# Two stages of one kernel rewritten: the order of pair attention's weights (with two memory tiles for them), and the Fourier stage's last part with sums in PSUM and fixed instruction orders

## The chip, the cores and the metric

The kernel runs on one core of a Trainium2 chip. The metric is the device time of one execution in microseconds (us). All data is float32. An engine name is short for: PE = TensorE (matrix products), PEld = its weight loads, DVE = VectorE, ACT = ScalarE, POOL = GpSimd, SP = SyncE, which here only issues DMAs.

## What is computed

A network of four layers on x of shape (4, 64, 64, 128); each layer adds a "conv" part and an "ffn" part to x. The change touches the conv part of layer 2 (a Fourier operator with attention) and of layer 3 (pair attention). Of layer 2, the lines that matter come after its attention; each of the 4 x 128 planes of 64 x 64 is handled alike:

```python
p = _fno_layer(av, Pcw, Psw, H, W)                  # inverse transform of the attention's spectrum + skip
a = _inorm(p + xa, attn_w, attn_b)
an = _inorm(a, norm2_w, norm2_b)
m = _fno_layer(an, m0cw, m0sw, H, W, inner_norm=True, act=True)   # transform, filter, inverse, norm, + skip, gelu
m = _fno_layer(m, m1cw, m1sw, H, W, inner_norm=True, act=False)
out = _inorm(m, mon_w, mon_b) + a
```

Layer 3's conv part, for each of 4 images, with p and pn of shape (64, 64, 4 heads, 32):

```python
scores = einsum('bxahd,bayhd->bxayh', pn, pn) / sqrt(HD)
att = softmax(scores, axis=2)
x_upd = _layernorm(einsum('bxahd,bayhd->bxayhd', p, p), ln_g, ln_b)
agg = einsum('bxayh,bxayhd->bxyhd', att, x_upd)
```

The kernel never forms x_upd. For each (x, a, y, head) it makes one weight: exp(score - max) times the reciprocal root of the variance of p p, which is a product of squares minus the square of a product.

## The kernel before

The program is a list of tile operations in Python. A scheduler orders each engine's instructions by its own estimate of readiness, with the program's order as priority. Where the program says `issue_after` (the helper `k.turn`, L44; a local `turn` in pair attention's `combine`, L2849), an instruction is tied behind the last one that was so tied on the same engine, and the order is the written one. Operations issued through such a helper all carry its line (L2851 for `combine`).

**The Fourier stage's last part** (L2018 to L2305) works in 16 groups of eight tiles of 128 x 128: four groups for each of four images. A group is a Python generator, `group(b, g, pT)`, which gives way (`yield`) 28 times; two of these steps make a round, so it lives for 14 rounds. A new group starts every four rounds, so that three or four are alive at a time, and within a round the alive ones take turns, in an order that a sort key sets. I call four rounds a cycle; step n below is the n-th stretch between yields.

- Steps 0 to 3: the skip part `sk` is loaded by DMA (L1654), ACT makes the normalised input `xa` (L2173), POOL adds it to `sk` (L2195). PE makes the inverse transform of the spectrum `pT` (L2200, tile `pi`), ACT copies it out (`ir`, L2059), PE applies the second factor (L2066, tile `pf`, matrix `dya`), and DVE adds `pf` to `sk` (L2207).
- Steps 4 to 6: PE transforms `sk` (L2079, `prf`; L2090, `pz`), DVE takes `bn_stats` of it (L2127), a small product `pm` (L2135) sums them over partitions, DVE makes moments (L2137 to L2142), ACT the root (L2149).
- Step 7, `filtered`: for each of two halves, DVE makes four products of `pz` with the filter (L2101) and adds pairs of them (L2106, 66 x 1024).
- Steps 8 to 11, `back` and `inverse`: PE multiplies by `rx` (L2116, two products for each of eight tiles), ACT copies (`ir`), PE applies `dyq` (L2066, `pf`), DVE takes stats.
- Steps 12 to 15: moments, `mix` (L2183, DVE), gelu on ACT (L2173), transform of the result `y` (L2079), and `sk` scaled (L2173) and added to x (POOL, L2178).
- Steps 16 to 23: the same once more with the second filter. Steps 24 to 27: last moments, scale (ACT, L2173), add to x (POOL, L2178).

`warm` (L2044) gives PE products whose results are overwritten: three ahead of each `back`, two ahead of each `transform`, ten a group. At the first group of an image, `groups()` (L2279) turns the image's spectrum: 64 transposes of 64 rows (L2287) and eight ACT copies (L2288) into `pT`. PSUM's eight banks are three of tag `pr` (`pi`, `prf`, `pz`, `ptp`), four of `pf`, one of `pm`.

**Pair attention** (`stage_pair_attention`) runs for each image b: `project` (makes pT, pn and p2), `weights`, `combine`. In `weights`, `products(hp, src)` gives PE, for one pair of heads, four blocks of 32 small products, each block into two PSUM banks (L2760). For both pairs: products of pT are squared by ACT (L2769), products of p2 have the squares subtracted by DVE (L2772), and POOL clips them (L2773). Then ACT takes Ln of all four tiles `rs` and then Exp of all four (L2775, L2777). Then for each pair in turn: products of pn (scores), copied by ACT (L2786), a running maximum on DVE (L2788, L2793), a swap of halves on PE (`pmx`, L2795), subtraction on DVE (L2798), Exp on ACT (L2799), sums on PE (`pz`, L2804), then by halves g of the columns the product with `rs` on DVE (L2809) and the write to the DRAM tile `wd` (L2811, SP and ACT queues); last the sums' reciprocals (L2816, L2817). `combine` starts with `load_right(0)` and `load_right(1)`, which read halves 0 and 1 of `wd` back in another layout (L2840, tiles `R`); its 128 steps (`spread`, `gather`) follow, each with a product S of `L` and `R` on PE.

## Time and profile before

| | |
|---|---|
| time, median of 3 runs | 6426.42 us (6424.67 to 6432.6) |
| the profiled execution | 6428.93 us; span of its instructions 6427.1 us |
| mean granted TensorE clock | 0.901 |
| busy share of the span | PE 86%, DVE 72%, ACT 45%, POOL 32% |
| Fourier stage, last part | about 3246 to 3931 us of the span |
| pair attention, weights (first product of pT to first S) | 4340.5 to 4449.2, 4789.3 to 4899.0, 5236.4 to 5346.7, 5683.9 to 5792.9 us |

In a row of the groups view, the columns are line, engine, operation, tiles (out<-in), shapes, count | busy us and mean ns of one | idle time of the engine just before, and what ended it. A row of the timeline is start us, length us, engine, line, operation, tiles, count, and in brackets the idle time before it. A float32 product is recorded as two MATMULs and two LDWEIGHTS. The windows view gives, for each stretch, its length, then busy us and count of each engine, the granted clock (PEclk, 1.00 is full speed), and DMA load.

### The profile page before, as it was taken

How to read it: one execution, taken by the hardware profiler on the slowest of the kernel's cores; microseconds unless marked ns; L12 is line 12 of the kernel's file. 1: busy time of each engine (PE TensorE's matmuls, PEld its weight loads, DVE VectorE, ACT ScalarE, POOL GpSimd, SP SyncE). 2: the span in 40 equal slices, each digit the busy share in tenths (PEclk: the TensorE clock that was granted, in tenths of full speed). 3: DMA queues.
4: the chain of work that ended last, by engine and by line, in shares of the span. 5: the costliest groups of instructions: out<-in, count | busy, mean ns of one | idle time of the engine just before them, and what ended most of it. 6: DMA issues, size and time to landing. Idle time of an engine off the chain costs nothing. (4 is left out here: it accounts for less than half of the span.)

```text
span 6427.1 us, 143768 instructions
## 1 busy us (share of the span) xinstructions
PE 5532.0 (86%) x57327; PEld 2990.1 (47%) x57327; DVE 4619.2 (72%) x9921; ACT 2906.9 (45%) x6599; POOL 2078.0 (32%) x1828
## 2 busy tenths in 40 slices
PE   8978888866688779979999987988998998989999
PEld 4446666644465555324455553334243252252233
DVE  7868787844477644859978887765866857847877
ACT  5635555533154323740045555753343352352375
POOL 0012222210000121008932212534654644635545
PEclk9989888977799889999988897997997988979999
DMA  6667888880400013049810000011111112111101
GB/s 171 181 181 209 238 241 245 244 243 5 174 1 1 2 38 94 1 136 186 182 28 14 14 7 6 1 33 39 39 45 46 39 37 53 38 49 44 34 20 33
DMA packets 714228, 545.16 MB, mean 85 GB/s; under 512 B 299872, under 2 KB 625000, under 8 KB 710216
## 3 DMA queue, kind: packets, MB, share of 16 engines
q1 hardware_dynamic: 669096, 491.03, 28.3%
q10 hardware_dynamic: 44448, 44.78, 2.2%
q8 instruction: 458, 7.50, 0.5%
q14 instruction: 226, 1.85, 0.1%
HBM read 366.25 MB, written 152.86 MB: 81 GB/s over the span
## 5 line engine op out<-in xcount | busy, mean ns | idle before, releaser
L2851 DVE TENSOR_TENSOR t<-S,q 128x1536 f32<-128x1536 f32 x512 | 893.6, 1754 | 174.5 <-PE S L2851 172.7
L2851 POOL TENSOR_TENSOR t<-t,q 128x512 f32<-128x512 f32 x512 | 651.6, 1273 | 490.3 <-ACT t L2851 489.2
L2851 ACT COPY t<-S 128x512 f32<-128x512 f32 x512 | 299.7, 585 | 827.8 <-PE S L2851 751.3
L2851 PE MATMUL S<-R,L 32*128 32x512 f32 x4096 | 612.7, 652 | 44.4 <-DMA R<-wd 39.3
L2851 PE MATMUL acc<-t,sum 128*32 128x512 f32 x4096 | 548.1, 608 | 0.6 <-DVE t L2851 0.5
L2567 PE MATMUL pe<-ew,yT 128*128 128x512 f32 x1024 | 491.0, 616 | 27.2 <-DVE xs L2573 24.8
L937 DVE COPY_PREDICATED band<-bit,band 128x384 f32<-128x384 int32 (+11 forms) x384 | 312.5, 924 | 171.1 <-ACT band L928 151.7
L918 PE MATMUL S<-kpad,qm 32*64 32x192 f32 (+3 forms) x8192 | 351.1, 393 | 80.1 <-ACT band L928 29.4
L2573 DVE SCALAR_TENSOR_TENSOR xs<-pe,gate,xs 128x128 f32<-128x128 f32 x1024 | 331.3, 344 | 96.8 <-PE pe L2567 81.9
L2851 PEld LDWEIGHTS S<-R,L 32*128 32x128 f32 x4096 | 179.1, 186 | 462.4 <-ACT t L2851 391.4
L1989 PE MATMUL acc<-w,attT 128*64 128x396 f32 x2048 | 348.2, 500 | 25.6 <-issue 15.0
L2576 ACT ACTIVATE sc<-pe,gate 128x128 f32<-128x128 f32 x1024 | 290.3, 377 | 162.3 <-PE pe L2567 139.5
L1985 DVE TENSOR_TENSOR w<-xp,e 128x1188 f32<-128x1188 f32 x256 | 336.0, 1385 | 33.2 <-ACT xp L1968 14.6
L1029 PE MATMUL pt<-ident,D 128*128 128x128 f32 x1536 | 261.4, 320 | 65.5 <-DMA D<-dd 49.9
L918 PEld LDWEIGHTS S<-kpad,qm 32*64 32x64 f32 x8192 | 253.0, 147 | 136.6 <-issue 66.8
L2567 PEld LDWEIGHTS pe<-ew,yT 128*128 128x128 f32 x1024 | 183.8, 195 | 267.6 <-issue 172.3
L1984 POOL TENSOR_TENSOR w<-xtl,e 128x396 f32<-128x396 f32 x256 | 260.4, 1033 | 116.6 <-DMA e<-ed 73.3
L1031 ACT COPY dt<-pt 128x512 f32<-128x512 f32 x384 | 204.4, 595 | 138.1 <-PE pt L1029 137.7
L2851 PEld LDWEIGHTS acc<-t,sum 128*32 128x32 f32 x4096 | 81.6, 108 | 392.3 <-issue 366.9
L1445 POOL TENSOR_TENSOR xs<-xs,zT 128x512 f32<-128x512 f32 x32 | 39.5, 1269 | 682.4 <-DVE zT L1444 682.0
L1989 PEld LDWEIGHTS acc<-w,attT 128*64 128x64 f32 x2048 | 159.9, 137 | 214.1 <-issue 145.8
L1029 PEld LDWEIGHTS pt<-ident,D 128*128 128x128 f32 x1536 | 215.8, 204 | 87.2 <-DMA D<-dd 53.9
(545 smaller groups left out, 11727.8 us busy)
## 6 DMA issues: line engine op xcount, KB each, us to landing
vb<-vd SPq DMA_DIRECT2D x272, 256.0 KB
e<-ed SPq DMA_DIRECT2D x64, 792.0 KB
D<-dd SPq DMA_DIRECT2D x128, 192.0 KB
D<-dd SPq DMA_DIRECT2D x128, 168.0 KB
D<-dd SPq DMA_DIRECT2D x128, 144.0 KB
w<-in_e_weight_dram ACTq DMA_DIRECT2D x16, 1024.0 KB
w<-in_e_weight_dram SPq DMA_DIRECT2D x16, 1024.0 KB
D<-dd SPq DMA_DIRECT2D x128, 120.0 KB
```

The lines of the kernel that those rows point to most:

```text
L918: ins = nc.tensor.matmul(acc[g][64 * h : 64 * h + 64].rearrange("p (a s) c -> p a s c", a=3), qm[rows, h, m, :], keys, start=(m == 0), sto ...
L937: nc.vector.copy_predicated(flat[:, :, 0:n], bit[:, 0, :, i : i + 1].to_broadcast([128, 48, n]), flat[:, :, s : s + n])
L1029: ins = nc.tensor.transpose(pt[:, g, :], D[:, g, ty : ty + 382 : 3], k.ident)
L1031: nc.scalar.copy(dt, pt)
L1445: nc.gpsimd.tensor_tensor(k.xs[b][:, 4 * g : 4 * g + 4, :], k.xs[b][:, 4 * g : 4 * g + 4, :], s, op=ALU.add)
L1984: nc.gpsimd.tensor_tensor(w[:, 3:4], planes[q][:, 3:4], wide(1, [[132, 3], [1, 132]]), op=ALU.mult)
L1985: nc.vector.tensor_tensor(w[:, 0:3].rearrange("p b c m -> p b (c m)"), xp[:, q % 2], wide(3, [[1, 396]]), op=ALU.mult)
L1989: nc.tensor.matmul(acc[b // 2][64 * (b % 2) : 64 * (b % 2) + 64].rearrange("p c m -> p (c m)"), attT[:, b // 2, hp, 64 * (b % 2) : 64 * (b ...
L2567: nc.tensor.matmul(pe[h].rearrange("p e c -> p (e c)"), yT[:, 128 * t : 128 * t + 128], ew[:, 4 * h : 4 * h + 4, :].rearrange("p e c -> p ...
L2573: nc.vector.scalar_tensor_tensor(xt, pe[0][:, e, :], gate[:, t, e : e + 1], xt, op0=ALU.mult, op1=ALU.add)
L2576: nc.scalar.activation(sc[:, e, j, :], pe[1][:, e, :], AF.Copy, scale=gate[:, t, 4 + e : 5 + e])
L2851: last[engine] = f(*args, **kw)
```

## The change

In the Fourier part, every PE, ACT and DVE instruction now goes through `k.turn` or `k.vector`: each of these engines runs them in the order of the text. The order of the groups in a round is a table (`rank`). `sk` + `xa` + `pf` is summed in PSUM: two products with the identity follow the one with `dya` in the same bank, and ACT copies the sum into `sk`; POOL's and DVE's additions are gone. In the second half of each filter the addition L2106 is gone, and PE adds four products in place of two. Of the ten `warm` products four are left. The spectrum is turned by pieces of 32 rows (`turned`), a half piece at the end of each cycle, two ahead of the first. The banks are four `pr`, three `pf`, one `pm`; `sk`, `m` and `ir` have one buffer less.

In pair attention, PE, ACT, DVE and the weights' DMAs also run in written order. Ln and Exp of the first pair's `rs` are taken while the second pair's products of p2 run; both pairs' scores come next, one after the other, with maxima, Ln and Exp of the rest between; the halves of the weights go to two DRAM tiles `wd[0]`, `wd[1]`, and `load_right(0)` is issued as soon as half 0 of both pairs is on its way, ahead of half 1 of the second pair.

```diff
@@ Fourier stage, last part
+            for engine in ("PE", "ACT", "DVE"):
+                k.last.pop(engine, None)
+            product = lambda *args, **kw: k.turn("PE", nc.tensor.matmul, *args, **kw)
+            activate = lambda *args, **kw: k.turn("ACT", nc.scalar.activation, *args, **kw)
+            copy = lambda *args: k.turn("ACT", nc.scalar.copy, *args)
...
+            def last_of_inverse(r, dyi, n=0, more=()):
+
+                pf = ps.tile([128, 4, 128], F32, tag="pf", name="pf", bufs=3)
+                warm(pf, n)
+                product(pf, dyi, r, start=True, stop=not more)
+                for i, t in enumerate(more):
+                    product(pf, k.ident, t, start=False, stop=i == len(more) - 1)
+                return pf
...
-                    if h < 2:
-                        nc.vector.tensor_tensor(m[:, :, 0], m[:, :, 0], m[:, :, 1], op=ALU.add)
+                    if h < 1:
+                        k.vector("tensor_tensor", m[:, :, 0], m[:, :, 0], m[:, :, 1], op=ALU.add)
...
-                    products = [(u, c) for u in range(2) for c in range(1 if h < 2 else 2)]
+                    products = [(u, c) for u in range(2) for c in range(1 if h < 1 else 2)]
...
-                return inverse(terms, dyq, 3)
+                return inverse(terms)
...
-                for h in range(2):
-                    h4 = slice(4 * h, 4 * h + 4)
-                    nc.gpsimd.tensor_tensor(sk[:, h4], sk[:, h4], xa[:, h4], op=ALU.add)
...
-                pfs = yield from inverse(terms, dya)
+                rs = inverse(terms)
+                yield
+                apply(xa, lambda j: k.xs[b][:, 8 * g + j, :], rss[b][:, t8], nbs[b][:, t8])
+                yield
                 for h in range(2):
-                    h4 = slice(4 * h, 4 * h + 4)
-                    nc.vector.tensor_tensor(sk[:, h4], sk[:, h4], pfs[h], op=ALU.add)
+                    pf = last_of_inverse(rs[h], dya, 0, (half(sk, h), half(xa, h)))
+                    copy(half(sk, h), pf)
                 yield
-                rs = transform(sk, 2)
+                yield
+                rs = transform(sk, 1)
...
+            def turned(p, a):
+                if a == 0:
+                    pTs[p] = bp_.tile([66, 2, 32, 32], F32, tag="pT", name="pT", bufs=2)
+                b, r0 = p // 2, 64 * (p // 2 % 2) + 32 * (p % 2)
+                rows = slice(r0, r0 + 32)
+                for y0 in (0, 16):
+                    pt = ps.tile([66, 16, 32], F32, tag="pr", name="ptp", bufs=4)
+                    for j in range(16):
+                        k.turn("PE", nc.tensor.transpose, pt[:, j, :], ph[rows, b // 2, 32 * a + y0 + j, :], k.ident[rows, rows])
+                    copy(pTs[p][:, a, :, y0 : y0 + 16].rearrange("p n y -> p y n"), pt)
...
-                active.sort(key=lambda a_: {13: 0, 7: 12}.get(a_[1], a_[1]))
+            rank = {n: i for of in ((8, 4, 0, 12), (13, 5, 1, 9), (6, 2, 10), (3, 11, 7)) for i, n in enumerate(of)}
...
+                active.sort(key=lambda a_: rank[a_[1]])
                 for _ in range(2):
                     for a_ in active:
                         next(a_[0])
+                if rounds % 4 == 3 and n < 14:
+                    turned(n // 2 + 1, n % 2)
@@ pair attention, the end of weights()
+            for _ in scores(0):
+                pass
+            second = scores(1)
+            next(second)
+            next(second)
+            for r in rs[2:4]:
+                turn("ACT", nc.scalar.activation, r, r, AF.Ln, bias=k.eps5)
+            maxima(0)
+            for _ in second:
+                pass
+            powers(0)
+            for r in rs[2:4]:
+                turn("ACT", nc.scalar.activation, r, r, AF.Exp, scale=-0.5)
+            maxima(1)
+            powers(1)
+            totals(0)
+            for g in range(2):
+                leave(0, g)
+            totals(1)
+            leave(1, 0)
+            load_right(0, wd, R[0], turn)
+            leave(1, 1)
+            R.append(sixteen("X1", [8, 8, 64], "R1"))
+            nc.gpsimd.memset(R[1], 0.0)
+            load_right(1, wd, R[1], turn)
+            for hp in range(2):
...
@@ DRAM tiles
-            wd = dr.tile([4, 4, 64, 16, 64], F32, tag="wd", name="wd")
+            wd = [dr.tile([4, 4, 64, 8, 64], F32, tag=f"wd{g}", name=f"wd{g}") for g in range(2)]
```

`scores`, `maxima` (running maximum to subtraction), `powers` (Exp), `totals` (sums on PE) and `leave` (product with `rs` and the writes) hold the steps of the loop over `hp` as it was.

## The prediction

> **What bounds the kernel now.** I read the page first (its chain of waits ends in the last layer and says nothing of the two stages), then the windows view over the cycles of the Fourier part, cut where each group's product with `dya` starts:

> ```profile
> 3349.90:3398.90 49.00, 44.59 (x244) 31.29 (x242) 35.55 (x118) 30.19 (x61) 8.44 (x6) 0.79 0.04 12
> 3436.60:3474.30 37.70, 34.82 (x180) 22.39 (x178) 35.54 (x118) 21.49 (x50) 7.70 (x6) 0.91 0.05 15
> 3511.90:3559.90 48.00, 42.38 (x242) 29.47 (x241) 35.71 (x118) 30.99 (x63) 7.69 (x6) 0.86 0.04 12
> 3761.10:3798.60 37.50, 33.46 (x179) 21.40 (x178) 35.04 (x118) 18.51 (x41) 5.16 (x4) 0.95 0.01 1
> sum 486.30, PE 438.93 PEld 288.79 DVE 427.57 ACT 273.00 POOL 91.78; mean PE 36.58 PEld 24.07 DVE 35.63 ACT 22.75 POOL 7.65
> ```

> Twelve full cycles take 486.3 us, 40.5 each: nine of 37.5 to 39.1, in which DVE is busy 35 (93%), and three of 48 to 49, where a new image is turned and DVE waits. DVE sets the pace. The groups view of two plain cycles (3761 to 3836) gives the prices:

> ```profile
> L2116 PE MATMUL pi<-rx,w 66*128 66x128 f32 x128 | 14.9, 275 | 0.0
> L2173 ACT ACTIVATE m<-m,sh,c 128x128 f32<-128x128 f32 x32 | 12.8, 483 | 0.0
> L2106 DVE TENSOR_TENSOR w<-w 66x1024 f32<-66x1024 f32 x8 | 9.7, 1214 | 0.0
> L2207 DVE TENSOR_TENSOR sk<-sk,pf 128x512 f32<-128x512 f32 x4 | 2.7, 676 | 0.0
> ```

> For pair attention I read the timeline of the first image's weights. ACT takes Ln and Exp of all `rs` ahead of the first score copy, the second pair comes wholly after the first, and S waits for the last write:

> ```profile
> 4386.17 4.06 ACT L2775 ACTIVATE rs<-rs,eps 128x2048 f32<-128x2048 f32 x2 [3.67 <-POOL rs L2773]
> 4391.54 3.71 ACT L2777 ACTIVATE rs<-rs 128x2048 f32<-128x2048 f32 x2
> 4395.16 3.97 ACT L2786 COPY s<-po 128x512 f32<-128x512 f32 x8
> 4406.98 8.52 PE L2804 MATMUL pz<-s,both 128*128 128x512 f32 x16
> 4415.43 6.11 PE L2760 MATMUL po<-pn 32*64 32x64 f32 x162
> 4438.22 2.30 DVE L2809 TENSOR_TENSOR s<-s,rs 128x1024 f32<-128x1024 f32 x2
> 4444.57 5.13 SPq L2840 DMA_DIRECT2D R<-wd  x8
> 4449.23 2.09 PE L2851 MATMUL S<-R,L 32*128 32x512 f32 x8 [10.33 <-DMA R<-wd]
> ```

> The same timeline prices one recorded half of a 512-column product, at half clock (0.85 us from start to start) and at full (0.43):

> ```profile
> 4408.00 0.34 PEld L2804 LDWEIGHTS pz<-s,both 128*128 128x128 f32 x1 [0.52 <-issue]
> 4408.85 0.34 PEld L2804 LDWEIGHTS pz<-s,both 128*128 128x128 f32 x1 [0.52 <-issue]
> ...
> 4410.62 0.19 PEld L2804 LDWEIGHTS pz<-s,both 128*128 128x128 f32 x1 [0.24 <-issue]
> 4411.05 0.19 PEld L2804 LDWEIGHTS pz<-s,both 128*128 128x128 f32 x1 [0.24 <-issue]
> ```

> **Pair attention, worked along ACT, then PE and DVE (first image).** Until 4381 PE is full with products of pT and p2 (9 us for 256 records) and stays as it is. ACT ends its squares at 4373; a table load (1.28) and two Ln (4.2), a load and two Exp (4.1) fill the time to 4384. PE makes the scores, 4381 to 4390 and, with 1.9 us of waiting for the first pair's maxima, 4390 to 4401. ACT copies eight blocks behind PE to 4391, two more to 4393; load and Ln of the other `rs` (5.5) end at 4399, six copies at 4402, load and Exp of the first scores (5.3) at 4407, Exp of `rs` (4.0) at 4411, Exp of the second scores at 4415. DVE's maxima and subtractions (two of 1.0, four small, two of 2.3) are done at 4410.5 and hold nothing up. PE's sums start after the second swap, 4406.2: 8.5 us for the first pair, as in the row at 4406.98, then 16 x 0.43 = 6.9, to 4421.6. DVE's product for half 0 of the second pair ends at 4422.9. Before, the last product ended at 4440.5 and S began 8.7 us later (writes landed 4.1 later, then 4.7 for issue and landing of `R`). Half 0 keeps this distance: S at 4431.6, 17.6 earlier. Against that, `load_right(1)` now stands on ACT's queue behind the landing of `wd[1]` (about 4433.5, then four issues of 0.6), and `combine`'s first ACT copy behind it: up to 2.4 us. DVE's reciprocals end at 4430 and PSUM is free in time. I take 15.5 us an image; bounds 10 (sums at half clock throughout) to 17.6. Four images differ by under 2 us in the trace: **-62** (-40 to -70).

> **Fourier, what the engines do.** DVE loses two L2207 (0.68) and two L2106 (1.21): 35.1 - 3.8 = 31.4 a cycle. PE loses six fillers (12 x 0.43 = 5.2) and gains four products with the identity (8 x 0.43 = 3.4), 32 records of L2116 (at 0.117: 3.7) and 32 narrow transposes. A transpose of 32 columns isn't in the trace: the ones of 64 start 0.11 apart at half clock; bounds 0.03 to 0.11, I take 0.06, so 1.9 a cycle. The plain cycles' PE work without waits and half-clock time is 30.6 (sum over records, 0.43 or 0.112 each), so 34.4 after. ACT gains two copies and the turning (two of 1.08), 25 in all; POOL loses work. By these sums neither engine would need over 37.

> **Fourier, what the fixed order does.** But written orders make a ring. In a cycle's second round (groups at rounds 13, 5, 1, 9), ACT first scales the group at 13 (step 26), then copies the PSUM sums of the group at 1. These have only one `pf` bank: of three, two hold the group at 5 until `mix`, a round later. So the second half of the sum on PE waits for the first half's copy, the copy for the eight activations ahead of it, these for DVE's step 26, which stands behind `filtered` of round 8. Behind the sum on PE stands `back` of round 9, and behind that `pm` of round 6, from which DVE's next work starts. Once round:
> - DVE from step 12 to step 26: all but the stats of step 11 (2.6), 28.8; two roots on ACT in its way, 0.5 each; `pm` hand-overs 0.7; dependent small instructions now in a row instead of interleaved (some 0.2 apart at 3812 to 3814), 0.7: 31.2.
> - ACT: eight activations at 0.40 (3.2) and one copy (0.57): 3.8.
> - PE: three products of 0.86 (2.6), 48 records at 0.117 (5.6), `pm` (0.3): 8.5.

> 43.5 us a cycle, 3.0 above 40.5, with DVE idle for some 10. Bounds: 41.7, if fewer of DVE's small instructions are stretched by POOL's additions (single ones reach 1.2 us beside usual 0.15), to 45.2, if 3.4 us of the ring's PE work fall into half clock. Twelve cycles: **+36** (+14 to +56). Of the turning's three long cycles nothing is left; that gain lies in the 40.5. The first three cycles: the first is 10 us longer (PE's `back` of group 0, behind the whole filter, now stands ahead of group 1's inverse), the second 5 shorter, the third already the ring, 6 longer: +11. The end, without new groups, lacks the sum's part of the ring: -7 in two cycles. Together **+40** (+15 to +62).

> The trace grants 0.95 in plain cycles, whose longest PE wait is 1.9 us, and 0.79 to 0.86 where PE waits longer. [...]

> **Sum.** The profiled execution's own time, 6428.9, is 2.5 above the median: 6428.9 - 62 + 40 = 6406.9, or 6404 beside the median. What a measurement can tell from no change is 0.2%, 13 us.

> **Rivals.**
> - *The ring doesn't bind* (the scheduler gives the sum another bank, or step 26 comes early), and PE sets the pace at its 34.4 plus the 3 us that it loses now to waits and half clock: 37.4. Twelve cycles give -37, the ends -3: Fourier -40, total 6324. For it: DVE would be at 84%, and the three long cycles vanish. Against it: each link of the ring follows from an order or a bank count in the text.
> - *Slower: the clock in the ring.* PE idles ahead of the ring's 8.5 us; each microsecond of that work done at half clock adds one, and a longer cycle idles more. With all 8.5 at half clock a cycle would be 52, the total 6509; with half of them 47.7 and 6456, which I give. It decides from 1.9 us more a cycle, a stretch of 3.7 us, where pair attention's gain is used up. For it: half-clock stretches of 3.4 to 6.8 us stand in every plain cycle now. Against: PE is 79% busy in the ring.
> - *The order in pair attention moves the wait only*: S then waits for half 1's writes and `R` of both halves in one queue, 4440 instead of 4431.6, gain 9 an image, total 6430.

> **How the numbers follow.** The forecast (ring at about 43.5 and pair attention -62) has 0.52; its own range is 6385 to 6428. The first rival has 0.25, the second 0.15, the third 0.08. Faster by over 0.2% (below 6413.5): 0.7 of the forecast's 0.52, all of the first rival: 0.61. Within: 0.25 of 0.52 and a fifth of the other two: 0.17. Slower: 0.22. The range leaves out the lower part of the first rival and the upper of the second: 6320 to 6452.

> **What would show it.** Right: DVE near 31 busy of 43 to 44 a cycle; PE's longest wait for the ACT copy of `sk`, that copy's for the group at 13; S some 15 us earlier after the first product of pT; score copies ending near 4402. Wrong: cycles under 39 (the ring isn't there), PEclk under 0.85 in them (second rival), or S released by half 1's writes (third).

## The result, and the profile after

The changed kernel takes **6512.33 us** (median of 4 runs, 6509.41 to 6521.92) against 6429.51 for the kernel before on the same chip: ratio 1.0131, interval 1.0113 to 1.0149, 83 us slower where 6404 was forecast. The profiled execution's span is 6510.9 us (6427.1 before), the mean granted clock 0.893 (0.901).

The two halves of the change go opposite ways. The weights phases of pair attention (first product of pT to first S) take 92.2, 93.9, 94.4 and 93.2 us, 64 less in all. The Fourier stage's last part takes 832 us in place of 688. The windows view over the same twelve cycles as before, three of them and the sum:

```profile
3425.80:3477.10 51.30, 44.97 (x237) 32.13 (x236) 31.60 (x113) 25.04 (x54) 5.09 (x4) 0.80 0.04 11
3578.90:3628.70 49.80, 44.12 (x237) 31.56 (x236) 31.61 (x113) 25.20 (x54) 5.10 (x4) 0.81 0.04 11
3829.60:3879.30 49.70, 45.28 (x237) 32.04 (x236) 32.73 (x113) 25.13 (x53) 5.06 (x4) 0.77 0.04 12
...
sum 597.30, PE 532.32 PEld 378.12 DVE 383.08 ACT 300.57 POOL 61.02; mean PE 44.36 PEld 31.51 DVE 31.92 ACT 25.05 POOL 5.08
```

49.8 us a cycle, before 40.5. DVE is down to 31.9 as the edits meant, but now it is busy only 64% of the cycle. PE is up to 44.4. The granted clock of 0.80 over the twelve cycles (0.77 to 0.82 in the full ones) tells why PE's time grew beyond its new work: at half clock for 2 x (1 - 0.80) = 0.4 of the cycle, 20 us. The groups view of two of these cycles (3678 to 3778) says the same by durations:

```profile
L46 PE MATMUL pi<-rx,w 66*128 66x128 f32 x192 | 32.2, 349 | 0.5 <-ACT pT L46 0.5
L46 ACT ACTIVATE m<-m,sh,c 128x128 f32<-128x128 f32 x32 | 12.7, 480 | 2.0 <-DVE sh L46 2.0
L46 DVE TENSOR_TENSOR w<-w 66x1024 f32<-66x1024 f32 x4 | 4.9, 1222 | 0.1
```

The filter additions are halved (x8 to x4), `back` has 192 records in place of 128, and the mean of one rose from 275 to 349 ns. The waits view of eleven cycles names the waits that matter:

```profile
DVE mv L46 <- PE pm L46: 158.1, 22, 11.8
DVE r L46 <- ACT d L46: 30.1, 22, 2.4
PE pz L46 <- DVE w L46: 24.6, 11, 2.2
PE pf L46 <- ACT sk L46: 20.9, 11, 2.6
```

DVE waits 14 us a cycle for `pm`, in two waits; PE waits for a bank that DVE's filter frees, and for ACT's copy of the sum. One cycle in the timeline shows how they hang together (`pm` of round 6 ends at 3691.6 and again at 3741.4):

```profile
3691.62 0.19 DVE L46 TENSOR_REDUCE mv<-pm 128x16 f32<-128x32 f32 x1 [9.02 <-PE pm L46]
3708.52 1.86 PE L46 MATMUL pz<-fr,fwp 128*66 128x512 f32 x2 [2.24 <-DVE w L46]
3710.17 10.57 PE L46 MATMUL pi<-rx,w 66*128 66x128 f32 x48
3718.46 2.47 DVE L46 TENSOR_TENSOR w<-pz,f 66x512 f32<-66x512 f32 x4
3720.66 3.68 PE L46 MATMUL pi<-ra,pT 66*64 66x128 f32 x32
3724.93 3.19 ACT L46 ACTIVATE xa<-xs,nb,rstd 128x128 f32<-128x128 f32 x8
3724.98 0.19 DVE L46 TENSOR_REDUCE mv<-pm 128x16 f32<-128x32 f32 x1 [4.04 <-PE pm L46]
3728.34 0.20 DVE L46 RECIPROCAL r<-d 128x8 f32<-128x8 f32 x1 [2.37 <-ACT d L46]
3729.31 3.19 ACT L46 ACTIVATE m<-m,sh,c 128x128 f32<-128x128 f32 x8 [1.00 <-DVE sh L46]
3732.40 0.56 ACT L46 COPY sk<-pf 128x512 f32<-128x512 f32 x1
3733.01 1.12 PE L46 MATMUL pf<-ir,dya 128*128 128x512 f32 x2 [1.56 <-ACT sk L46]
3741.41 0.19 DVE L46 TENSOR_REDUCE mv<-pm 128x16 f32<-128x32 f32 x1 [10.13 <-PE pm L46]
```

The ring of the forecast is there from the ninth row on: step 26's activations, the copy, the second half of the sum, `back` of round 9, `pm`, DVE. But DVE comes to step 26 late. PE stood 2.24 us ahead of the second half of the second spectra; its next 48 products of `back` (group at round 4) take 10.57 us, 0.22 each, and the inverse 3.68. `pm` of round 12 stands behind both in PE's order, so DVE, done with its filter at 3720.94, waits 4.04 for it. ACT's copies of the late inverse push the eight activations of `xa` back, and the root stands behind those: 2.37 more.

Pair attention, first image, timeline (before: the rows at 4386 to 4449 shown above):

```profile
4533.35 4.28 ACT L2783 ACTIVATE rs<-rs,eps 128x2048 f32<-128x2048 f32 x2
4540.92 1.07 ACT L2783 COPY s<-po 128x512 f32<-128x512 f32 x2 [1.16 <-PE po L2783]
4545.33 15.45 PE L2783 MATMUL pz<-s,both 128*128 128x512 f32 x32
4566.41 2.77 SPq L2783 DMA_DIRECT2D R<-wd  x4
4569.29 1.65 SPq L2783 DMA_DIRECT2D wd<-s  x2
4571.23 2.09 PE L2924 MATMUL S<-R,L 32*128 32x512 f32 x8 [10.44 <-DMA R<-wd]
```

Counted from the end of ACT's squares (4373 before, 4512.2 after), the last score copy ends at +29.8 (forecast +29), the sums run from +33.1 to +48.6 (+33.2, +48.6), S starts at +59.0 (+58.6). It is released by `R` of half 0, which is queued ahead of half 1's last writes.

### The profile page after: what moved, and what is told of

Read it like the earlier page. It is cut to its first block, busy times and chain, and to the rows that moved or that the text cites. A ratio compares the mean times of both kernels' runs of the same rounds, so it can differ in the third digit from the quotient of the medians.

```text
span 6510.9 us, 145095 instructions
## 1 busy us (share of the span) xinstructions
PE 5646.0 (87%) x58031; PEld 3101.2 (48%) x58031; DVE 4551.9 (70%) x9857; ACT 2939.3 (45%) x6631; POOL 2033.8 (31%) x1796
## 5 line engine op out<-in xcount | busy, mean ns | idle before, releaser
L1985 DVE TENSOR_TENSOR w<-xp,e 128x1188 f32<-128x1188 f32 x256 | 336.0, 1385 | 33.2 <-ACT xp L1968 15.9
L1029 PE MATMUL pt<-ident,D 128*128 128x128 f32 x1536 | 263.3, 321 | 59.0 <-DMA D<-dd 42.6
L46 PEld LDWEIGHTS pi<-rx,w 66*128 66x128 f32 x1536 | 251.0, 259 | 37.9 <-ACT pT L46 19.3
L46 PE MATMUL pi<-rx,w 66*128 66x128 f32 x1536 | 254.7, 346 | 12.1 <-ACT pT L46 5.5
```

The source lines that it names most:

```text
L46: self.last[engine] = r = f(*args, **kw)
L1029: ins = nc.tensor.transpose(pt[:, g, :], D[:, g, ty : ty + 382 : 3], k.ident)
L1985: nc.vector.tensor_tensor(w[:, 0:3].rearrange("p b c m -> p b (c m)"), xp[:, q % 2], wide(3, [[1, 396]]), op=ALU.mult)
```

## The experiments

Ratios are to the kernel before on the same chip, with their intervals; its median lay between 6426.7 and 6430.3 us in all of these comparisons, so that times of different runs can be set side by side to some 4 us.

**One half of the change at a time.** e1 is the kernel before with the new pair attention (`weights`, `load_right`, `wd`), its Fourier part untouched; e2 is the changed kernel with the old pair attention. Two places of e1's diff (it also holds the rest of `weights` and `load_right`); that of e2 is the same reversed, against the changed kernel:

```diff
-            turn = [0]
+            count, last = [0], {}
+            def turn(engine, f, *args, **kw):
+                with tc.issue_after(last[engine].ins) if engine in last else ExitStack():
+                    last[engine] = f(*args, **kw)
...
-            wd = dr.tile([4, 4, 64, 16, 64], F32, tag="wd", name="wd")
+            wd = [dr.tile([4, 4, 64, 8, 64], F32, tag=f"wd{g}", name=f"wd{g}") for g in range(2)]
```

> The kernel before with pair attention's new weights alone. All theories: the start of S comes 16 us earlier in each of four images (the changed kernel's profile: 92.1 to 94.3 us from the first product of pT to the first S, against 108.7 to 110.3), so 64 us less than the kernel before, 6360 to 6370. If some of the loss of the whole change lay outside the Fourier part (layers that follow, DMA), it would be above 6375.

> The kernel before with the Fourier part's change alone. If the two parts add up: 64 us more than the changed kernel, 6570 to 6580, with cycles of 49 to 52 us. If they interact: off by more than 10 us from that.

Pair attention alone: 6368.59 us, 0.9902 (0.9878 to 0.9925), 62 us faster. Fourier alone: 6565.04, 1.0206 (1.0184 to 1.0229), 135 slower, 49.8 us a cycle. The Fourier part alone is 53 us above the whole change, where 64 was expected if the two add up: 5 us below the stated range. The sum of the two, +73, still lies within the interval of the +83 of both. So the loss is in the Fourier part, to within these 10 us.

**The fillers back in their old places (e3).** Ten a group, as before the change: three ahead of each `back`, two ahead of each `transform`.

```diff
-            def inverse(terms):
+            def inverse(terms, n=0):
...
+                    warm(pi, n if h == 0 else 0)
...
-                return inverse(terms)
+                return inverse(terms, 3)
...
-                rs = transform(sk, 1)
+                rs = transform(sk, 2)
...
-                pfs = [last_of_inverse(r, dyq, 1 - h) for h, r in enumerate(rs)]
+                pfs = [last_of_inverse(r, dyq) for r in rs]
```

> The changed kernel with the ten fillers of before in their old places (three ahead of each back, two ahead of each transform; none ahead of the dyq products). Clock theory (the loss beyond the ring is PE's half clock, which the fillers ahead of back had kept away): granted clock in the cycles from 0.80 to over 0.90, cycles of 43 to 45 us though PE has 5 us more to do, total 6425 to 6450. Order theory (the written order costs 9 us a cycle whatever the clock): cycles stay at 49 to 52, total 6500 to 6530. Load theory (PE has too much to do): cycles get longer by up to 5 us, total 6530 to 6590.

6523.3, 1.0142 (1.0120 to 1.0164): no faster. One cycle in the windows view, then two places of PE in it in the timeline:

```profile
3685.00:3736.20 51.20, 43.30 (x250) 27.73 (x249) 32.74 (x113) 25.08 (x54) 5.06 (x4) 0.93 0.04 11
```

```profile
3695.91 2.74 PE L46 MATMUL pi<-ph,ident 128*128 128x512 f32 x6
3698.48 5.52 PE L46 MATMUL pi<-rx,w 66*128 66x128 f32 x48
...
3721.11 1.07 PE L46 MATMUL pz<-fr,fwp 128*66 128x512 f32 x2 [2.25 <-DVE w L46]
3722.72 4.24 PE L46 MATMUL pi<-ph,ident 128*128 128x512 f32 x6 [0.53 <-ACT pT L46]
3726.79 5.52 PE L46 MATMUL pi<-rx,w 66*128 66x128 f32 x48
```

The clock is back at 0.93 and `back` at 5.5 us. I first read this as the clock being worth nothing. The rows say otherwise: the fillers stand ahead of `back`, on the path. Behind the gap of 2.25 us six records take 4.24 us, where the half clock had cost 5.1 on `back`; at the other place, in the ring, they add 2.6. The cure took what it gave, so this run could not separate clock and order.

**Free order.** The changed work and banks, without any tie in the Fourier part (e4).

```diff
-            product = lambda *args, **kw: k.turn("PE", nc.tensor.matmul, *args, **kw)
+            product = nc.tensor.matmul
-            activate = lambda *args, **kw: k.turn("ACT", nc.scalar.activation, *args, **kw)
+            activate = nc.scalar.activation
...
-                    k.vector("bn_stats", st[:, j, :], src(j))
+                    vector("bn_stats", st[:, j, :], src(j))
```

> The changed kernel without the written order in the Fourier part: the same operations, banks and table, but the scheduler orders PE, ACT and DVE as it did before. Order theory: cycles fall to 38 to 41, total 6370 to 6400. Clock theory: PE still has few fillers; clock in the cycles stays at 0.80 to 0.85, cycles 43 to 48, total 6420 to 6480. Bank theory (three banks for pf and four for pr make the waits, whatever the order): cycles stay at 49 to 52.

6331.78, 0.9845 (0.9823 to 0.9866): 181 us faster than the changed kernel. The mean cycle is 37.1 us, less than the 38 to 41 of the order theory. Two of its cycles in the windows view:

```profile
3583.50:3619.10 35.60, 34.32 (x238) 24.62 (x237) 28.85 (x115) 24.36 (x53) 5.29 (x4) 1.00 0.06 16
3690.40:3735.50 45.10, 43.80 (x238) 32.14 (x237) 30.89 (x124) 24.38 (x53) 5.30 (x4) 0.78 0.04 13
```

The PSUM sums, the new banks and the thinned fillers are thus no loss by themselves (against e1, which has the old Fourier part, the time is 37 us lower); the written order is. Two of the twelve cycles take 9.4 us longer than the others, with the same instructions and one long stretch at half clock (20.5 us): that is what such a stretch is worth in this order.

**Fillers where PE idles anyway (e5).** The changed kernel with all its orders, and two fillers in `pm`'s bank between the halves of the second spectra.

```diff
-            def spectra(rs):
+            def spectra(rs, n=0):
                 pzs = []
                 for r in rs:
+                    if n and pzs:
+                        warm(ps.tile([128, 512], F32, tag="pm", name="pmw", bufs=1), n)
...
-                pm = ps.tile([128, 48], F32, tag="pm", name="pm", bufs=1)
+                pm = ps.tile([128, 512], F32, tag="pm", name="pm", bufs=1)[:, :48]
...
-                pzs = spectra(rs)
+                pzs = spectra(rs, 2)
```

> The changed kernel, orders and all, with two fillers (512 columns, into the bank of pm) between the two halves of the second spectra of each group, where PE stands 2.2 us for a bank just before each 20 us stretch at half clock. Nothing is added ahead of any back. Theory 'order, and the clock inside it': the gap closes, the half-clock stretch does not start, back of round 4 takes 5.5 us instead of 10.6 and the inverse 2.1 instead of 3.7; DVE no longer waits 4 us for pm of round 12, and the root behind the xa scaling comes without its 2.4 us. The ring is then the forecast's: 43.5 to 45.5 us a cycle, against 49.8. Twelve cycles of about -5 and some in the first three: 6430 to 6460 us. Theory 'order alone' (the ring's length does not depend on the clock, as ten fillers in their old places seemed to say: 51.2): 49 to 50 a cycle, 6500 to 6520. Theory 'clock needs more than a closed gap' (the 66-row products themselves let it fall): half clock stays near 20 us a cycle, 6500 to 6520.

6457.32, 1.0048 (1.0029 to 1.0066), 55 us less than the changed kernel. The copy of the sum, and the place of the fillers, in the timeline:

```profile
3646.99 0.56 ACT L46 COPY sk<-pf 128x512 f32<-128x512 f32 x1
3647.61 2.08 PE L46 MATMUL pf<-ir,dya 128*128 128x512 f32 x2 [4.52 <-ACT sk L46]
...
3673.27 1.88 PE L46 MATMUL pmw<-ph,ident 128*128 128x512 f32 x4
3675.67 1.07 PE L46 MATMUL pz<-fr,fwp 128*66 128x512 f32 x2 [0.52 <-DVE w L46]
3677.28 5.62 PE L46 MATMUL pi<-rx,w 66*128 66x128 f32 x48 [0.54 <-ACT pT L46]
3682.84 1.97 PE L46 MATMUL pi<-ra,pT 66*64 66x128 f32 x32
```

`back` is at 5.6, the inverse at 2.0, and DVE finds `pm` of round 12 ready. The cycle is 45.6 us, clock 0.93 to 0.96. Now the ring of the forecast stands alone: PE's longest wait is the 4.52 us for the copy of `sk`, behind which the first two records of the sum's second half take 2.08 us in place of 1.12, at half clock.

**One engine's order at a time.** Free order, with the ties put back on PE only (e6), on ACT only (e7), on DVE only (e8). The edit for DVE, the others likewise:

```diff
-            vector = lambda f, *args, **kw: getattr(nc.vector, f)(*args, **kw)
+            vector = k.vector
```

> The kernel with free order (6332, 37.1 us a cycle), with the written order put back on PE alone; ACT and DVE as the scheduler likes. Theory 'the ring needs all three engines' orders': PE's order is nearly the one that the scheduler found, except that back of round 9 starts between the halves of the sum; 36 to 40 us a cycle, 6320 to 6370. Rival 'PE's order is the cause' (back and pm stand behind the second half of the sum): 46 us or more a cycle, 6450 or more.

> The kernel with free order, with the written order put back on ACT alone. Theory 'the ring needs all three': the root stays behind the xa scaling and the copy of the sum behind step 26, 2 to 3 us, part of it hidden: 36 to 41 us a cycle, 6320 to 6380. Rival 'ACT's order is the cause': 46 us or more, 6450 or more.

> The kernel with free order, with the written order put back on DVE alone. Theory 'the ring needs all three': DVE's dependent small instructions stand in a row again (some 2 us) and it stands before pm with other work ready behind: 38 to 43 us a cycle, 6350 to 6410. Rival 'DVE's order is the cause' (it stands ten microseconds before pm whatever the others do): 46 us or more, 6450 or more.

PE's order: 6343.96, 0.9867 (0.9850 to 0.9883), 37.4 us a cycle. ACT's: 6477.69, 1.0069 (1.0048 to 1.0090), 46.6. DVE's: 6424.35, 0.9994 (0.9981 to 1.0007), 42.6. "All three are needed" falls: against 37.1 with none, ACT's order alone costs 9.5 us a cycle, three quarters of the 12.7 that all three cost, DVE's 5.5 (its time is 14 us above the range expected), and PE's next to nothing (0.3). The three come to 15.3, more than the 12.7, so they overlap in part; and with DVE's order the granted clock falls too, to 0.75 to 0.94 in the full cycles. One place of PE in the timeline with ACT's order alone:

```profile
3654.99 3.17 ACT L46 ACTIVATE sk<-sk,sh,s 128x128 f32<-128x128 f32 x8
3658.07 1.92 ACT L46 COPY pT<-ptp 66x512 f32<-66x512 f32 x2
3659.14 10.61 PE L2122 MATMUL pi<-rx,w 66*128 66x128 f32 x48 [3.34 <-ACT pT L46]
```

The copies that free a bank for PE stand behind eight activations of `sk`; PE waits 3.34 us and then runs `back` at half clock, in 10.61 us. With the gap fillers added:

> Free order but for ACT's written order (6478, 46.6 us a cycle, 18.8 of it at half clock), and the two fillers in pm's bank between the halves of the second spectra. PE stands 0.7 and 3.3 us there, the longer one for the copies of pT behind the eight activations of sk on ACT. Theory 'ACT's order costs through the clock as well': the first gap is closed, but the second is behind the fillers and stays; so half clock falls only if the first counts: 42 to 44 us a cycle if it does (6410 to 6440), 46 to 48 if the 3.3 us gap alone starts the stretch (6465 to 6485). Rival 'ACT's order costs by its waits alone': 46 to 48, with the half clock gone.

6449.77, 1.0037 (1.0024 to 1.0051), 44.8 us a cycle, the clock at 0.84 (about 14 us of a cycle at half). None of the three expectations holds: the fillers close the first gap only; the one for `pT` stays, at 2.2 us, and of the 18.8 us at half clock some 14 are left. How ACT's 9.5 us divide into waits and clock stays open.

**The forecast's link by itself.** On top of the gap fillers (e10), one rank is moved, so that ACT copies the sum ahead of step 26.

```diff
-... (13, 5, 1, 9) ...
+... (5, 1, 13, 9) ...
```

> The changed kernel with written orders and the fillers in the gap (6457, 45.6 us a cycle), and one rank moved: in the second round the groups go 5, 1, 13, 9 instead of 13, 5, 1, 9. On ACT the copies of the sum then stand ahead of the eight activations of step 26; on PE and DVE nothing else changes place in that round. Theory 'the forecast's ring' (copy behind step 26 behind DVE): the copy of the first half starts when PE has made it, 4.0 to 4.5 us earlier, PE's gap of 4.5 us and the half clock behind it go too: 40 to 42 us a cycle, 6390 to 6415. Rival 'it is only one of several chains of like length' (PE's own order from back to pm, DVE behind pm): 44 to 45.5 a cycle, 6440 to 6455.

6379.74, 0.9928 (0.9913 to 0.9944), 78 us less than with the fillers alone. Windows view, then the link in the timeline:

```profile
3449.90:3489.80 39.90, 36.95 (x241) 25.01 (x240) 31.58 (x114) 25.25 (x54) 5.06 (x4) 1.00 0.05 14
```

```profile
3452.75 0.59 ACT L46 COPY sk<-pf 128x512 f32<-128x512 f32 x1 [0.26 <-PE pf L46]
3453.39 1.12 PE L46 MATMUL pf<-ir,dya 128*128 128x512 f32 x2 [0.72 <-ACT sk L46]
3456.75 3.18 ACT L46 ACTIVATE m<-m,sh,c 128x128 f32<-128x128 f32 x8
```

PE's wait falls from 4.52 to 0.72 us, the clock is full all through, and the mean of the twelve cycles falls by 6.0 to 39.7, just below what the forecast's ring led me to expect. And the move without the fillers:

> The changed kernel with the rank move alone (5, 1, 13, 9 in the second round), without the fillers in the gap. With both edits a cycle fell from 49.8 to 39.7, with the fillers alone to 45.6. Theory 'two chains side by side': while the half clock stays, PE's own chain (second spectra, back at 10.6 us, inverse 3.7, product with dyq 3.7, sum, back) is about as long as the one through step 26, so that the copy moved alone gives 0.5 to 2 us: 48 to 49.3 a cycle, 6490 to 6510. Rival 'the two costs add': the move alone is worth the 6 us that it was worth beside the fillers: 43.5 to 45, 6435 to 6460. Should the move alone end the half-clock stretch, 39.7 to 41 and 6380 to 6400.

6483.68, 1.0077 (1.0060 to 1.0094), 47.8 us a cycle. The four cells are 49.8 (neither), 47.8 (move), 45.6 (fillers), 39.7 (both): 2.0 and 4.1 alone, 10.1 together; the move alone gave slightly more than the 0.5 to 2 us expected, and its time lies 6 us below the range for it. The costs do not add: with the half clock, PE's own chain (spectra at 3708.52, `back`, inverse, `dyq`, to the end of the sum's first half at 3731.46) reaches the copy only 0.9 us before step 26 does, so cutting one chain leaves the other.

**Free order with the gap fillers, and with less on PE.**

> The kernel with free order and, between the halves of the second spectra, the two fillers in pm's bank. In the kernel with free order alone ten of the twelve cycles take 35.6 to 36.0 us and two 45.0, each with one stretch of 20.5 us at half clock that starts behind the gap of 1.28 us before the second half of the spectra. Theory 'clock': with the gap filled those two cycles go down to 35.6 to 36.5 and the others stay; the two fillers (1.7 us) lie in the gap, 0.4 beside it: 6312 to 6322 us, the fastest so far. Rival 'the fillers are work on the engine that sets the pace' (PE is busy 35.9 of 37.1): each cycle grows by 1.7, the two long ones vanish: no gain, 6325 to 6340.

6319.70, 0.9830 (0.9816 to 0.9843). Its windows' sum:

```profile
sum 429.20, PE 429.20 PEld 304.73 DVE 349.90 ACT 291.77 POOL 62.29; mean PE 35.77 PEld 25.39 DVE 29.16 ACT 24.31 POOL 5.19
```

The long cycles are gone, as the theory 'clock' had it; PE is busy all the time and sets the pace. The edit is that of the gap fillers, on e4. e12 then puts the second half of each filter back on DVE:

```diff
-                    if h < 1:
+                    if h < 2:
-                    products = [(u, c) for u in range(2) for c in range(1 if h < 1 else 2)]
+                    products = [(u, c) for u in range(2) for c in range(1 if h < 2 else 2)]
```

> Free order with the gap fillers, and the second half of each filter summed on DVE again, as before the change: DVE gets two additions of 1.21 us a cycle, PE loses 32 records of 0.117 (3.7 us). Theory 'with free order PE sets the pace' (36 busy of 37): 33 to 34.5 us a cycle, 20 to 30 us less than the same kernel with both sums on PE: 6285 to 6300. Rival 'a chain through all engines sets it': the addition stands in that chain, 36 to 38 a cycle, 6315 to 6340.

**6299.72, 0.9802 (0.9787 to 0.9817)**, the fastest of all: 127 us below the kernel before. The time is at the upper end of what was expected, the cycle is not: it fell only to 35.1, with PE busy 33.3 and DVE 32.0. By then neither has much slack, and which chain holds the last 2 us is open. Part of the gain, about 7 us, lies in the first three cycles (stage start to the fourth cycle 103.3 us in place of 109.9).

## Why the prediction was wrong

**Pair attention, -62: right.** -64 by the four phases, -62 by e1, and each time along ACT, PE and DVE within 1 us of the working. The third rival (S released by half 1) did not come.

**Fourier, what the engines do: right.** DVE 31.4 forecast, 31.9 measured. PE 34.4: in e9 PE is busy 35.8 us a cycle without a break, 1.7 of it the two added fillers, so 34.1.

**The ring: its links were right, one term of its length was not.** Forecast 31.2 on DVE from step 12 to step 26, 3.8 on ACT, 8.5 on PE. Measured in the cycle shown: 3691.62 to 3729.27, 37.7; then 3.7 to the end of the copy at 3732.96; then 8.4 to `mv` at 3741.41. The term that failed is 'DVE from step 12 to step 26', by 6.5 us. It holds 6.8 us of waits where I had allowed 1.7 (two roots of 0.5, `pm` 0.7): 4.04 for `pm` of round 12, 2.37 for the root behind `xa`, 0.37 for the other root. The other 1.4 is work; one small operation beside a POOL addition took 1.31 there. I checked what is queued ahead of the ring's own PE work, and not what PE has to do before `pm` of round 12 (`back` of round 4 and the new group's inverse, 7.5 us at full clock and 14.2 as it ran), nor what ACT has ahead of the root. e5 shows the size: with that PE work at full clock both waits vanish, the same stretch of DVE takes 31.5 (from `mv` at 3612.34 to step 26 at 3643.86, against the 31.2), and the cycle is 45.6, just over the bound of 45.2 that I gave the ring with some half clock in it. e10 shows that the link I named was then the bound: cut it, and 6.0 us go.

**Twelve cycles +36: measured +111** (12 x 9.25). **First three cycles +11:** the stage's start to the fourth cycle grew from 104.4 to 136.1, +32; with the clock kept (e5, 119.0) +15. **The end -7:** +1.5. Together +144 for the forecast's +40. Of the excess of 104, e5 returns 67 (stage 765 for 832).

**The second rival had the sign and nearly the extreme time (6509), from another place.** I let the half clock start in the ring's gap ahead of the second half of the sum and eat the ring's 8.5 us. In the cycle shown that work runs at full clock, and only in four of the twelve (those of 51.3 to 52.1 us) do 3.4 us of half clock fall into it. The long stretch starts behind a gap of 2.24 us that I had not seen, at the second spectra, and eats the work ahead of `pm` of round 12. That the times are so near is chance. The gap follows from the text too: with four `pr` banks and the order written, the second half waits until DVE has read the bank of the first filter's second half (`w`, ended 3708.46). In my bounds the half clock could take 3.4 us of the ring's PE work, 45.2 a cycle or 20 us in twelve cycles; what decided was not in that number but in which gap counted, and one of 2.24 us was enough. The kernel before shows that already: in its cycles of clock 0.95 the longest PE wait is 1.9 us, and one stretch of 3.4 us at half clock begins in it or just behind it. (Not all of its plain cycles have 0.95, as I wrote: three have 0.91 and one 0.87, and the longest of their half-clock stretches is 10.2 us, not 6.8.)

**The first rival** (PE sets the pace, 37.4 a cycle, 6324) is what the same work does once ACT and DVE are not tied: 37.1 and 6332 in e4, 35.8 and 6320 in e9.

## What to carry to other kernels

A written order is a bet on durations: before writing one, run the same work in free order, then tie one engine at a time; here the order of the least busy of the three, ACT at 25 us of a cycle, cost the most; in the place shown, copies that free PSUM banks stood behind eight activations whose results were needed later. Put fillers where the engine idles, in a bank that is free then, not ahead of the work they should speed up. Two costs that each seem worth 2 to 4 us may be worth 10 together when they sit on parallel chains, so test them together before dropping either.

## What the runs showed of the hardware

The granted clock fell to half at shorter gaps than I had reckoned with. In every full cycle of the changed kernel a half-clock stretch of 17.1 or 20.5 us began in the PE gap of 2.24 us ahead of the second spectra or at most 1.8 us behind its end; in two of the eleven full cycles of e4 one of 20.5 us began behind a gap of 1.28 us; in e10, with 0.5 us left there, none did (clock 1.00). The length of the gap is not the whole of it: behind PE's wait of 1.17 us ahead of `pm`, in every full cycle of the changed kernel and of e10, no stretch began, and in e4 the cycles with and without a stretch show the same rows with the same gap:

```profile
3453.84 1.07 PE L2094 MATMUL pz<-fr,fwp 128*66 128x512 f32 x2
3456.19 1.97 PE L2094 MATMUL pz<-fr,fwp 128*66 128x512 f32 x2 [1.28 <-ACT pT L2309]
3457.95 10.45 PE L2120 MATMUL pi<-rx,w 66*128 66x128 f32 x48
...
3606.44 1.07 PE L2094 MATMUL pz<-fr,fwp 128*66 128x512 f32 x2
3608.79 1.07 PE L2094 MATMUL pz<-fr,fwp 128*66 128x512 f32 x2 [1.28 <-ACT pT L2309]
3609.70 5.52 PE L2120 MATMUL pi<-rx,w 66*128 66x128 f32 x48
```

```profile
3452.68:3456.09 3.41, 2.23 (x34) 1.31 (x34) 3.41 (x9) 3.41 (x9) 2.29 (x2) 1.00 0.00 0
3456.09:3459.51 3.42, 3.32 (x10) 2.19 (x11) 3.42 (x15) 1.01 (x3) 0.50 (x1) 0.50 0.28 83
3609.70:3613.11 3.41, 3.41 (x32) 3.41 (x31) 3.41 (x17) 0.60 (x2) 0.00 (x0) 1.00 0.41 117
```

The 3.41 us up to 3456.09 hold nearly all of the gap, 32-row transposes and one pair of 512-column records (0.86 us at 0.43 each); the clock is 0.50 behind them. The 3.41 us up to 3609.70 hold the same gap and both pairs (1.7 us); the clock stays at 1.00. In the cycle of the changed kernel shown above, the 3.41 us up to 3708.64 hold the gap of 2.24 us and 1.17 us of work of PE, nearly all of it two records of 512 columns, and the clock is 0.50 behind them; those up to 3698.37 hold the wait of 1.17 us ahead of `pm` and 2.24 us of work, with four such records (1.88 us), and the clock stays at 1.00. What decides is not shown: no run here fixes a threshold.

A busy PE did not bring the clock back in the cycle shown as long as its products were narrow. `back` and the inverse (66 rows, at most 128 columns) ran without a break for 14 us at half clock, from 3710.17 on; the clock was back at 1.00 at 3729.12, behind 3.75 us of `dyq`'s products of 512 columns (from 3724.74). In e3, where six records of 512 columns followed the same gap (2.25 us), `back` behind them was at full clock, 5.52 us.
